# Layer 3 of a four-layer graph network: the pair's factors become the stationary operand of the sum over sources

## The chip, the cores and the metric

The kernel runs on one core of a Trainium2 chip. The metric is the device time of one execution in microseconds. A core has a matrix engine (TensorE, PE in the profile, with PEld for its weight loads), a vector engine (VectorE, DVE), a scalar engine for activation functions (ScalarE, ACT), a general engine (GpSimd, POOL), and queues that start DMA transfers (SP's above all). TensorE multiplies a stationary operand, loaded first (LDWEIGHTS), by a moving operand that is passed through it column by column; the result goes to PSUM, and the other engines read it from there.

## The reference

Four graph layers follow each other, each of the form x = x + layer(relu(layernorm(x)), adj), with 3327 nodes, 64 features and a dense 3327 x 3327 matrix adj in f32. Layer 0 is a gated recurrent layer applied twice, layer 1 a hyperbolic linear one, layer 2 a sum with weights that halve from neighbour to neighbour. The change is in layer 3:

```
x_tan = _logmap0(x, C)
left = x_tan @ att_W[:D] + att_b
right = x_tan @ att_W[D:]
adj_att = sigmoid(left + right.T) * adj
x_local = _logmap(x[:, None, :], x[None, :, :], C)
support_t = einsum('ij,ijd->id', adj_att, x_local)
return _proj(_expmap(x, support_t, C), C)
```

For target i and source j the term `_logmap(x_i, x_j)` is a factor that depends on the pair (i, j), times a combination of x_i and x_j. So the sum over j needs, for each target, two things: the factors times 64 features of x_j, and the factors times one number for each source.

## The kernel before

Nodes are padded to 3328, 26 blocks of 128. The first 13 blocks and the last 13 are kept side by side. Layers 0 to 2 come first (lines 142 to 485) and are not touched. Layer 3 works on **pairs**: `pairs` lists 26 of them, 13 for each half of the targets. A pair is one half of the targets (1664 of them, HN) and two blocks of sources, block c and block 13 + c, named b = 0 and b = 1. What is made for a pair is a tile `gl` of 128 sources by 2 x 1664 targets, f32: the pair's factors.

For each pair the engines do this. `load3` fetches the pair's part of adj (SP's queue). `distances(n, k)` runs on TensorE for half k of the targets: the two source blocks use the upper and the lower 64 rows of the array, and a bf16 matmul adds further terms. ScalarE then takes Gelu of the result into `gl` (L818) and Tanh for the attention into `th` (L825). `weights` multiplies by adj on VectorE (L845). `squares` is split between ScalarE (L836) and VectorE (L837). `products` multiplies both on VectorE in three pieces (L854), the first of which makes the whole of `gl[:, 0]`. Then comes the sum over sources on TensorE, in two functions. `gather` has the 64 features of a source block, scaled (`xd`), as its stationary operand and passes the factors, 416 targets at a time; the result has features on partitions and targets in columns, and two of them lie on the two halves of a PSUM bank (`accx0`, `accx1`). `gather_p` does the same with one column, `p2c`, and puts four rows into `accp`. Both add over the 13 pairs of a half.

After the last pair of a half, `collect` copies these sums into `half` (ScalarE and VectorE), turns them with 13 transposes on TensorE so that targets lie on partitions, and multiplies by `qs` into `sums`. `finish` then does the rest for that half on VectorE, with small steps; its steps for the first half are spread, four at a time, over the following pairs.

The order on each engine in layer 3 is the order in which the program writes the instructions (`manual_schedule`). The loop at lines 921 to 944 writes it by hand: for pair n, products of n, distances of n+1 (second half), gather of n, weights and squares of n+1, distances of n+2 (first half), gather_p of n. `gl` has three buffers, `th` and the tile of adj two; the PSUM tiles of the distances, `pta` and `ptb`, have one each.

Of the kernel before, what the change touches and what calls it, by code (L numbers as in the profile page):

```python
# [8 lines left out]
F32 = mybir.dt.float32  # L9
BF16 = mybir.dt.bfloat16  # L10
I32 = mybir.dt.int32
AF = mybir.ActivationFunctionType
OP = mybir.AluOpType
# [4 lines left out]
D = 64  # L18
P = 128
NB = 26  # L20
NP = NB * P
HB = NB // 2
HN = NP // 2
CH = 416
NQ = HN // CH
# [18 lines left out]
HG = -7.090763495839726  # L44
HK = 0.012618748686465375
HD = 0.7055609776434136 / HK
SQ = HN + 512


# [11 lines left out]
def gnn_kernel(ctx: ExitStack, tc: tile.TileContext, t, out):  # L61
    nc = tc.nc
    V, S, G, T = nc.vector, nc.scalar, nc.gpsimd, nc.tensor
# [7 lines left out]
    ident = const.tile([P, P], F32, name="ident")  # L71
# [9 lines left out]
    def small(pool, name):  # L81
        return pool.tile([P, NB], F32, name=name, tag=name)
# [59 lines left out]
    with ExitStack() as c012:  # L142
# [5 lines left out]
        ps_acc = c012.enter_context(tc.tile_pool(name="ps_acc", bufs=1, space=PSUM))  # L148
        pools = {}

        def scratch(name):
            return pools["ps"].tile([P, 512], F32, name=name, tag="ps")
# [42 lines left out]
        for n in ("1", "2"):  # L195
# [3 lines left out]
            b = nd.tile([P, 2, 3], F32, name="b" + n)  # L199
# [57 lines left out]
        def accumulators():  # L257
            return [ps_acc.tile([P, 512], F32, name=f"acc{q}", tag=f"acc{q}") for q in range(NQ)]
# [36 lines left out]
        with tc.tile_pool(name="gate", bufs=2) as gp:  # L295
            src = dst = h_t
            for (w, ih, hh, b, brz), order in zip(ggc, (UP, DOWN)):
# [3 lines left out]
                for q in range(NQ):  # L301
                    cs = slice(q * CH, (q + 1) * CH)
                    gates = []
                    for g in range(2):
                        p = scratch("gate")
# [10 lines left out]
                    n = gp.tile([P, CH], F32, name="n", tag="n")  # L316
# [72 lines left out]
        with ExitStack() as c2:  # L389
# [21 lines left out]
            for i in range(3):  # L411
                p = mk.tile([P, NB, D], BF16, name=f"part{i}", bufs=1)
# [6 lines left out]
            acc = accumulators()  # L419
            with tc.tile_pool(name="psc", bufs=2, space=PSUM) as psc, tc.manual_schedule():  # L420
# [19 lines left out]
                for j in reversed(range(NB)):  # L440
                    a = adj_block(j)
                    mask = mk.tile([P, NP], BF16, name="mask", tag="mask")
                    V.tensor_scalar(mask, a, 0.0, None, op0=OP.not_equal)  # L443
                    for k in range(NQ // 2):
                        ws = []
                        for h in range(2):
                            p = psc.tile([P, 2, 512], F32, name="cnt", tag="cnt")
                            for i in range(2):
# [3 lines left out]
                                    lhsT=tri,  # L452
                                    rhs=mask[:, i0 : i0 + CH],
                                    start=True,
                                    stop=behind is None,
                                )
                                if behind is not None:
                                    T.matmul(  # L458
                                        p[:, i, :CH],
                                        lhsT=ones,  # L460
                                        rhs=behind[:, i0 : i0 + CH],
                                        start=False,
                                        stop=True,
# [39 lines left out]
    n3 = c3.enter_context(tc.tile_pool(name="n3", bufs=1))  # L503
# [108 lines left out]
    sums = n3.tile([P, NB, D + 1], F32, name="sums")  # L612

    with ExitStack() as cf:
        f3 = cf.enter_context(tc.tile_pool(name="f3", bufs=1))
        wk = cf.enter_context(tc.tile_pool(name="wkf", bufs=2))
        ps_acc = cf.enter_context(tc.tile_pool(name="ps_accf", bufs=1, space=PSUM))
        ps = cf.enter_context(tc.tile_pool(name="psf", bufs=1, space=PSUM))
# [5 lines left out]
        pairs = [(hf, c) for hf in range(2) for c in range(HB)]  # L624
# [26 lines left out]
        last = f3.tile([P, 1], I32, name="last")  # L651
# [8 lines left out]
        q = small(n3, "q")  # L660
        V.tensor_scalar(q, x2, 0.5, -0.5, op0=OP.mult, op1=OP.add)
        V.reciprocal(q, q)
        xd = f3.tile([P, HB, 3, D], F32, name="xd")
# [10 lines left out]
        for n, (dst, a) in enumerate(((xs, 0), (xw, 1))):  # L674
            for c0 in range(0, HB, 8):
                m = min(8, HB - c0)
                p = pair_tile(n + c0 // 8).rearrange("p a b -> p (a b)")
# [38 lines left out]
        for i in range(3):  # L716
            b = f3.tile([P, 4, NB], BF16, name=f"part{i}")
# [20 lines left out]
        p = ps.tile([P, 1024], BF16, name="tr", tag="tr")  # L738
# [9 lines left out]
        for g in range(7):  # L748
            src = packt[:, g * P : (g + 1) * P]
# [9 lines left out]
        for i in range(4):  # L759
            p = pair_tile(i)  # L760
# [5 lines left out]
                p[:, :, :CH],  # L766
            )

        p2c = small(n3, "p2c")
        V.tensor_scalar(p2c, q, 2.0, 2.0, op0=OP.mult, op1=OP.add)  # L770
        qs = small(n3, "qs")
        V.tensor_scalar(qs, q, 0.125 * HK, None, op0=OP.mult)

# [3 lines left out]
        p = ps.tile([P, 512], F32, name="tr", tag="tr")  # L777
# [6 lines left out]
        gs, ths = {}, {}  # L784
# [48 lines left out]
        def squares(n):  # L833

            gl = gs[n].rearrange("p b n -> p (b n)")
            S.activation(gl[:, :SQ], gl[:, :SQ], AF.Square, bias=hg)  # L836
            V.scalar_tensor_tensor(  # L837
                gl[:, SQ:], gl[:, SQ:], 2 * HG, gl[:, SQ:], op0=OP.add, op1=OP.mult
            )
# [9 lines left out]
        def products(n):  # L849

            gl = gs[n].rearrange("p b n -> p (b n)")
            th = ths.pop(n).rearrange("p b n -> p (b n)")
            for lo, hi, hd in ((0, HN, HD), (HN, SQ, HD), (SQ, 2 * HN, HD + HG * HG)):
                V.scalar_tensor_tensor(  # L854
# [2 lines left out]

        acc = {}

        def gather(n):  # L860
            hf, c = pairs[n]
            if c == 0:
                for k in range(2):
                    acc[k] = ps_acc.tile([P, 512], F32, name=f"accx{k}", tag=f"accx{k}")
                acc["p"] = ps_acc.tile([P, 512], F32, name="accp", tag="accp")
            gl = gs[n]
            for b in range(2):
                first, last = c == 0 and b == 0, c == HB - 1 and b == 1
                for i in range(NQ):
                    T.matmul(  # L870
                        acc[i // 2][(i % 2) * D : (i % 2 + 1) * D, :CH],
                        lhsT=xd[:, c, b, :],
                        rhs=gl[:, b, i * CH : (i + 1) * CH],
                        start=first,
                        stop=last,
                    )

        def gather_p(n):
            hf, c = pairs[n]
            gl = gs.pop(n)  # L880
            for b in range(2):
                first, last = c == 0 and b == 0, c == HB - 1 and b == 1
                kk = 2 * c + b
                for i in range(NQ):
                    T.matmul(  # L885
                        acc["p"][32 * i : 32 * i + 1, :CH],
                        lhsT=p2c[:, kk : kk + 1],
                        rhs=gl[:, b, i * CH : (i + 1) * CH],
                        start=first,
                        stop=last,  # L890
                    )

        def collect(hf):
            half = f3.tile([D + 1, HN], F32, name="half", tag="half")
            for i in range(NQ):
                cs = slice(i * CH, (i + 1) * CH)
                src = acc[i // 2][(i % 2) * D : (i % 2 + 1) * D, :CH]
                srcp = acc["p"][32 * i : 32 * i + 1, :CH]
                S.activation(half[:D, cs], src, AF.Copy)
                V.tensor_copy(half[D : D + 1, cs], srcp)  # L900
            for c0 in range(0, HB, 6):
                n = min(6, HB - c0)
                p = ps.tile([P, 512], F32, name="tr", tag="tr")
                for c in range(n):
                    T.transpose(
                        p[:, c * (D + 1) : (c + 1) * (D + 1)],
                        half[:, (c0 + c) * P : (c0 + c + 1) * P],
                        ident[: D + 1, : D + 1],
                    )
                V.tensor_mul(  # L910
                    sums.rearrange("p (c a) d -> p c a d", a=2)[:, c0 : c0 + n, hf, :],
                    p[:, : n * (D + 1)].rearrange("p (c d) -> p c d", d=D + 1),
                    qs.rearrange("p (c a) -> p c a", a=2)[:, c0 : c0 + n, hf, None].to_broadcast(
                        [P, n, D + 1]
                    ),
                )
# [4 lines left out]
        for n in range(-2, len(pairs)):  # L921
            if n >= 0:
                products(n)
            if 0 <= n + 1 < len(pairs):
                distances(n + 1, 1)
            if n >= 0:
                gather(n)
            if 0 <= n + 1 < len(pairs):
                weights(n + 1)
                load3(n + 3)  # L930
                squares(n + 1)
            if n + 2 < len(pairs):
                begin(n + 2)
                distances(n + 2, 0)
            if n >= 0:
                gather_p(n)
                if pairs[n][1] == HB - 1:
                    hf = pairs[n][0]
                    collect(hf)
                    final = finish(hf)  # L940
            for _ in range(4):
                next(final, None)
            if n == 0:
                ok = nc.values_load(within, min_val=0, max_val=1)
# [4 lines left out]
    with ExitStack() as cg:  # L949
# [3 lines left out]
        ps_acc = cg.enter_context(tc.tile_pool(name="ps_acc3", bufs=1, space=PSUM))  # L953
        ps = cg.enter_context(tc.tile_pool(name="ps3", bufs=2, space=PSUM))
# [42 lines left out]
        for hf in range(2):  # L997
# [6 lines left out]
            for b0 in range(0, HB, 4):  # L1004
                bs = blocks[b0 : b0 + 4]
                p = scratch3(b0 // 4)
                for i, b in enumerate(bs):
                    k = slot(b)
# [5 lines left out]
            acc = [ps_acc.tile([P, 512], F32, name=f"ac{q}", tag=f"ac{q}") for q in range(NQ)]  # L1014
# [69 lines left out]
            for g in range(len(groups) + 1):  # L1084
                if g < len(groups):
                    for j in groups[g]:
                        n = hf * NB + j + 2
# [10 lines left out]
            half = g3.tile([D + 1, HN], F32, name="half", tag="half")  # L1098
            for q in range(NQ):
                S.activation(half[:, q * CH : (q + 1) * CH], acc[q][: D + 1, :CH], AF.Copy)  # L1100
            for c0 in range(0, HB, 6):
                n = min(6, HB - c0)
                p = scratch3(c0 // 6)
                for c in range(n):
# [10 lines left out]
                    op0=OP.mult,  # L1115
# [50 lines left out]
```

## Time and profile before

| | |
|---|---|
| three runs | 920.04, 920.91, 924.06 us; median 920.91 |
| the profiled execution | 922.38 us, of which the span from first to last instruction is 920.6 |
| busy in the span | PE 720.2, PEld 339.6, DVE 519.6, ACT 356.3, POOL 9.5 us |
| mean granted TensorE clock | 0.899 of full |
| layer 3's pairs | about 633 to 895 us, then finish to the end |
| weights L845 | 52 instructions of 1.89 us |
| distances L799 (f32), L810 (bf16) | 416 and 208 recorded passes of 416 columns |
| gather L870, gather_p L885 | 416 recorded passes each of 416 columns |
| transposes in collect L905 | 26, mean 278 ns |

The busy time of a matmul is from its start to a modelled end, so matmuls that follow each other in a pipeline overlap in it: how long TensorE is held by one is read from the start of one to the start of the next. The granted clock is the share of full speed that TensorE was allowed.

### The profile page before, as it was taken

The numbers are of one execution on the slowest core, as the hardware profiler recorded it, in microseconds if no ns is written. First come the engines' busy times: TensorE is split into PE (matmuls) and PEld (weight loads), VectorE is DVE, ScalarE is ACT, GpSimd is POOL, SyncE is SP. The second block draws the span as 40 slices with busy tenths as digits, with TensorE's granted clock in tenths as the row PEclk, the third lists the DMA queues.
The fourth block names the chain that finished last, engine by engine and source line by source line (L and its number), as shares of the span: only waits on it lengthen the run. The fifth ranks groups of instructions, "written<-read, shape, count | busy, mean of one in ns | idle before, by whom it ended". The sixth has DMA issues, their size and how long they took to land.

```text
span 920.6 us, 9670 instructions
## 1 busy us (share of the span) xinstructions
PE 720.2 (78%) x4043; PEld 339.6 (37%) x4043; DVE 519.6 (56%) x618; ACT 356.3 (39%) x361; POOL 9.5 (1%) x18
## 2 busy tenths in 40 slices
PE   0999998998953999505999999115899997699970
PEld 0644445443431444203444445112344442244420
DVE  4200025000189000796676675862899998899986
ACT  0000011000022000111666665012899995799961
POOL 1000000000000000000000002000000000000000
PEclk9999999999985999856999999556999997899995
DMA  8999930997000599500688610300465562445501
GB/s 274 378 379 429 404 122 21 384 359 275 0 1 0 209 385 373 221 0 1 253 330 310 243 53 1 151 3 10 149 223 176 197 222 80 159 159 217 200 24 22
DMA packets 25345, 170.22 MB, mean 185 GB/s; under 512 B 9165, under 2 KB 9293, under 8 KB 16077
## 3 DMA queue, kind: packets, MB, share of 16 engines
q1 hardware_dynamic: 21718, 168.88, 48.1%
q10 hardware_dynamic: 3575, 0.64, 0.4%
q8 instruction: 33, 0.54, 0.2%
q14 instruction: 19, 0.16, 0.1%
HBM read 168.40 MB, written 0.85 MB: 184 GB/s over the span
## 4 chain that ended last, share of the span: by engine, by line
PE 62%; DVE 19%; DMA 10%; issue 4%; ACT 3%; ACTq 1%; POOL 0%; SPq 0%; DVEq 0%; POOLq 0%
PE acc L261 28%; PE pt L799 9%; PE accx L870 8%; DMA adj<-in_adjT 6%; PE cnt L450 4%; PE cnt L458 4%; PE accp L885 3%; DMA res<-in_adjT 3%; PE pt L810 2%; DVE sq L86 1%; DVE gl L854 1%; PE lin L245 1%; ACT gl L818 1%; DVE n L88 1%; DMA w<-in_W 1%
## 5 line engine op out<-in xcount | busy, mean ns | idle before, releaser
L261 PE MATMUL acc<-adj,m_n 128*64 128x416 f32 x816 | 203.8, 523 | 9.4 <-DMA adj<-in_adjT 8.8
L261 PEld LDWEIGHTS acc<-adj,m_n 128*64 128x64 f32 x816 | 85.4, 138 | 109.7 <-issue 90.3
L261 PE MATMUL acc<-res,m_n 128*64 128x416 f32 x432 | 108.0, 523 | 22.8 <-DVE m_n L349 22.2
L466 ACT ACTIVATE w<-cnt,ebias 128x832 uint16<-128x832 f32 x104 | 93.4, 950 | 62.9 <-PE cnt L458 51.8
L278 DVE COPY m_t<-acc 128x416 f32<-128x416 f32 x12 | 6.2, 582 | 189.1 <-PE acc L261 189.1
L845 DVE SCALAR_TENSOR_TENSOR th<-th,adj 128x1664 f32<-128x1664 f32 x52 | 97.7, 1887 | 12.5 <-ACT th L825 12.4
L799 PE MATMUL pt<-xs 64*128 64x416 f32 x208 | 99.4, 559 | 5.4 <-ACT gl L818 5.4
L799 PE MATMUL pt<-xw,xs 64*128 64x416 f32 x208 | 100.5, 565 | 0.0
L854 DVE SCALAR_TENSOR_TENSOR gl<-gl,th 128x1664 f32<-128x1664 f32 (+2 forms) x78 | 97.6, 1305 | 0.0
L870 PE MATMUL accx<-gl,xd 128*64 128x416 f32 x416 | 83.2, 539 | 13.8 <-DVE gl L854 13.8
L818 ACT ACTIVATE gl<-pt 128x832 f32<-128x832 f32 x104 | 84.1, 861 | 24.3 <-PE pt L810 24.3
L825 ACT ACTIVATE th<-leftb,righth 128x1664 f32<-128x1664 f32 x52 | 87.6, 1685 | 0.0
L450 PE MATMUL cnt<-mask,tri 128*128 128x416 bf16 x208 | 70.8, 344 | 2.4 <-ACT w L466 1.0
L261 PEld LDWEIGHTS acc<-res,m_n 128*64 128x64 f32 x432 | 44.5, 138 | 68.4 <-issue 66.5
L261 PE MATMUL acc<-w,part 128*64 128x416 bf16 x624 | 66.1, 346 | 4.3 <-DVE part L413 4.3
L458 PE MATMUL cnt<-behind,ones 128*128 128x416 bf16 x192 | 65.1, 339 | 0.0
L476 DVE TENSOR_TENSOR behind<-behind,mask 128x3328 bf16<-128x3328 bf16 x23 | 43.5, 1892 | 36.0 <-PE cnt L458 36.0
L217 PE MATMUL tr<-ident,h_n 128*128 128x128 f32 x26 | 6.0, 423 | 62.4 <-DVE h_n L139 62.4
L836 ACT ACTIVATE gl<-gl,hg 128x2176 f32<-128x2176 f32 x26 | 54.8, 2106 | 0.0
L870 PEld LDWEIGHTS accx<-gl,xd 128*64 128x64 f32 x416 | 30.8, 141 | 62.1 <-DVE gl L854 33.4
L810 PE MATMUL pt<-rows_i,rows_j 64*128 64x416 bf16 x208 | 50.8, 347 | 0.0
L443 DVE TENSOR_SCALAR mask<-adj 128x3328 bf16<-128x3328 f32 x21 | 39.5, 1885 | 19.9 <-DMA adj<-in_adjT 13.3
(228 smaller groups left out, 645.4 us busy)
## 6 DMA issues: line engine op xcount, KB each, us to landing
adj<-in_adjT SPq DMA_DIRECT2D x89, 1664.0 KB
res<-in_adjT SPq DMA_DIRECT2D x9, 1664.0 KB
xn<-in_x SPq DMA_DIRECT2D x1, 832.0 KB
out<-w SPq DMA_DIRECT2D x2, 416.0 KB
ih<-in_wihT ACTq DMA_DIRECT2D x4, 48.0 KB
hh<-in_whhT ACTq DMA_DIRECT2D x4, 48.0 KB
w<-in_W ACTq DMA_DIRECT2D x4, 16.0 KB
attw<-in_att_W SPq DMA_DIRECT2D x1, 64.0 KB
```

The source lines that it names most:

```text
L261: T.matmul(acc[q][h * D : (h + 1) * D, :CH], lhsT=lhsT, rhs=rhs, start=first, stop=last)
L450: T.matmul(p[:, i, :CH], lhsT=tri, rhs=mask[:, i0 : i0 + CH], start=True, stop=behind is None,)
L458: T.matmul(p[:, i, :CH], lhsT=ones, rhs=behind[:, i0 : i0 + CH], start=False, stop=True,)
L466: S.activation(w, p[:, :, :CH], AF.Relu, bias=ebias, scale=-EXP_UNIT)
L799: T.matmul(pts[b][:, i, :CH], lhsT=xs[rs, c * P : (c + 1) * P], rhs=rhs[rs, q0 : q0 + CH], start=True, stop=False,)
L810: T.matmul(pts[b][:, i, :CH], lhsT=rows_j[rs, j0 : j0 + P], rhs=rows_i[rs, i0 : i0 + CH], start=False, stop=True,)
L818: S.activation(gs[n][:, b, 2 * k * CH : (2 * k + 2) * CH].rearrange("p (i n) -> p i n", i=2), pts[b][:, :, :CH], AF.Gelu, scale=-HA,)
L825: S.activation(ths[n][:, k, :], leftb[:, hf * HN : (hf + 1) * HN], AF.Tanh, bias=righth[:, kk : kk + 1], scale=0.5,)
L836: S.activation(gl[:, :SQ], gl[:, :SQ], AF.Square, bias=hg)
L845: V.scalar_tensor_tensor(th[:, b, :], th[:, b, :], 1.0, a[:, b, :], op0=OP.add, op1=OP.mult)
L854: V.scalar_tensor_tensor(gl[:, lo:hi], gl[:, lo:hi], hd, th[:, lo:hi], op0=OP.add, op1=OP.mult)
L870: T.matmul(acc[i // 2][(i % 2) * D : (i % 2 + 1) * D, :CH], lhsT=xd[:, c, b, :], rhs=gl[:, b, i * CH : (i + 1) * CH], start=first, stop=last,)
```

## The change

A new tile `xp` holds for each source block the 64 features and, as a 65th column, the factor that was `p2c`. `gather` and `gather_p` are replaced by `sum_targets(n, b)`, called once for each source block of the pair, at the two places in the loop where they stood. It has 128 columns of the pair's factors (128 sources by 128 targets) as the stationary operand and passes the 65 columns of `xp`, 13 times for the 13 target blocks of a half. The result has targets on partitions. Seven target blocks share one PSUM bank (`accx0`), six the other (`accx1`); the start flag is given for the first block in each bank. `collect` has no copies and no transposes: it multiplies the two banks by `qs` into `sums`. The copy into `xp` is made by GpSimd.

```diff
-        p2c = small(n3, "p2c")
-        V.tensor_scalar(p2c, q, 2.0, 2.0, op0=OP.mult, op1=OP.add)
+        xp = f3.tile([P, NB, D + 1], F32, name="xp")
+        G.tensor_copy(
+            xp[:, :, :D].rearrange("p (c a) d -> p c a d", a=2), xd[:, :, :2, :]
+        )
+        V.tensor_scalar(xp[:, :, D], q, 2.0, 2.0, op0=OP.mult, op1=OP.add)
...
-        def gather(n):
...
-        def gather_p(n):
...
+        def sum_targets(n, b):
             hf, c = pairs[n]
-            if c == 0:
+            if c == 0 and b == 0:
                 for k in range(2):
...
+                    acc[k] = ps_acc.tile([P, BANK_BLOCKS, D + 1], F32, name=f"accx{k}", tag=f"accx{k}")
+            gl = gs[n] if b == 0 else gs.pop(n)
+            for i in range(HB):
+                T.matmul(
+                    acc[i // BANK_BLOCKS][:, i % BANK_BLOCKS, :],
+                    lhsT=gl[:, b, i * P : (i + 1) * P],
+                    rhs=xp[:, 2 * c + b, :],
+                    start=c == 0 and b == 0 and i % BANK_BLOCKS == 0,
+                    stop=c == HB - 1 and b == 1,
+                    skip_group_check=True,
+                )
 
         def collect(hf):
-            half = f3.tile([D + 1, HN], F32, name="half", tag="half")
...
+            for k in range(2):
+                cs = slice(k * BANK_BLOCKS, min(HB, (k + 1) * BANK_BLOCKS))
+                n = cs.stop - cs.start
                 V.tensor_mul(
...
+                    sums.rearrange("p (c a) d -> p c a d", a=2)[:, cs, hf, :],
+                    acc[k][:, :n, :],
...
             if n >= 0:
-                gather(n)
+                sum_targets(n, 0)
...
             if n >= 0:
-                gather_p(n)
+                sum_targets(n, 1)
```

## The prediction

> **What bounds the kernel now.** The change lies in layer 3, so the shares of the whole span say little. I read first the groups of instructions from 650 to 900 us with shapes kept apart, then the busy time by window, then the order of time of one pair, then the waits (from 660 to 756 us ACT waits 4.0 us in all for distances, DVE for nothing).
>
> The groups of the two gathers (columns: busy us, mean ns of one, idle before and what ended it):
>
> ```profile
> L870 PE MATMUL accx<-gl,xd 128*64 128x416 f32 x416 | 83.2, 539 | 13.8 <-DVE gl L854 13.8
> L870 PEld LDWEIGHTS accx<-gl,xd 128*64 128x64 f32 x416 | 30.8, 141 | 62.1 <-DVE gl L854 33.4 <-issue 28.3
> L885 PE MATMUL accp<-gl,p2c 128*1 128x416 f32 x416 | 41.0, 511 | 0.0
> ```
>
> 26 pairs times 8 matmuls are 208, but 416 are recorded: an f32 matmul is issued as two passes, each with its own weight load. Now the windows: one pair in the steady part, the middle of the layer, and a stretch of layer 0 (columns: length, then busy us of PE, PEld, DVE, ACT, POOL, granted clock, DMA share, GB/s).
>
> ```profile
> 60.00:120.00 60.00, 59.33 (x246) 25.72 (x243) 0.00 (x0) 0.00 (x0) 0.00 (x0) 1.00 0.99 411
> 705.13:713.75 8.62, 8.62 (x57) 3.68 (x56) 8.62 (x7) 8.26 (x8) 0.00 (x0) 1.00 0.57 203
> 763.40:773.80 10.40, 5.86 (x25) 3.06 (x25) 7.70 (x19) 5.37 (x9) 0.00 (x0) 0.67 0.41 155
> ```
>
> A pair takes 8.62 us, and DVE has no idle time in it: two weights (L845, 3.63 us), one square (L837, 1.27), three products (L854, 3.68), counted from start to start. ACT works 8.26 and waits 0.36. PE also shows 8.62, but that is latency; its streaming time must come from starts. These rows give them (start, length, engine):
>
> ```profile
> 713.78 3.03 PE L870 MATMUL accx<-gl,xd 128*64 128x416 f32 x16
> 716.74 0.61 PE L799 MATMUL pt<-xs 64*128 64x416 f32 x1
> 717.20 0.51 PE L799 MATMUL pt<-xs 64*128 64x416 f32 x1
> 717.55 0.34 PE L810 MATMUL pt<-rows_i,rows_j 64*128 64x416 bf16 x2
> 718.69 1.58 PE L885 MATMUL accp<-gl,p2c 128*1 128x416 f32 x16
> 720.20 0.61 PE L799 MATMUL pt<-xs 64*128 64x416 f32 x1
> ```
>
> From 717.20 to 717.55 is one f32 pass of 416 columns, 0.35 us. The gather holds PE from 713.78 to 716.74, 2.96 us for 16 passes: two run side by side (64 output rows each), 8 x 0.347 = 2.78 plus 0.18. The factor row holds it from 718.69 to 720.20, 1.51: four side by side, 4 x 0.347 = 1.39 plus 0.12. A half of the distances takes 1.95 where ACT does not hold it (716.74 to 718.69), with 1.73 of passes. So PE needs 2 x 1.95 + 2.96 + 1.51 = 8.37 of 8.62 us: **DVE bounds the pair, but PE has only 0.25 us to spare.** That is what the reader is to take from the rows: a near tie of three engines.
>
> **What the Trainium skill says.** TensorE: Matmul & The Clock Gate, section LDWEIGHTS, prices a weight load at columns / 1.2 ns, whatever the rows: 107 ns for 128 columns, 53 for 64. The trace agrees with this for f32: the first pass after a switch is followed by the next after 0.46 us where 128 columns are loaded (716.74 to 717.20), after 0.40 where 64 are, after 0.35 for one column; less the 0.35 of the pass, 0.11, 0.05 and 0. The same page, section Back-to-back issue gap, says that the spacing in a stream of load and matmul is set by both, overlapped; it has 81 ns at N=128, of no stated type. Here the trace differs and decides: layer 0's linear, f32, 128 columns loaded and 128 passed, at full clock, is
>
> ```profile
> 28.59 1.28 PE L245 MATMUL lin<-w,h_t 128*128 128x128 f32 x10
> ```
>
> (1.28 - 0.275 of the last) / 9 = 112 ns: load and pass lie on each other, neither is added. TensorEngine Tiling (Array Packing), section Key Properties, says that a change of tiling mode drains the array; I read the 0.12 left over in gather and factor row as that.
>
> **The change, part by part.** (1) Removed from every pair: 2.96 + 1.51 = 4.47 us of PE. (2) Added: 2 x 13 matmuls with 128 weight columns and 65 moving columns, so 52 loads and 52 passes. A pass of 65 columns is 0.347 x 65 / 416 = 54 ns, its load 107: the load is the longer, and no other tile of the array shares the time. That loads stay overlapped when they are longer than the pass is shown by the closing transposes, whose 128-column load goes through faster, with a pass of 65 columns:
>
> ```profile
> 898.50 0.45 PEld L905 LDWEIGHTS tr<-ident,half 65*128 65x128 f32 x6 [1.56 <-issue]
> ```
>
> (0.45 - 0.144) / 5 = 61 ns[...]. I take 112 ns for each of the 26 passes in a call of sum_targets, plus 0.12 drain and 0.11 for the first load, which nothing hides: 2.90 + 0.23 = **3.1 us a call**. Bounds: 107 ns and the drain alone, 2.9; 125 ns (a few more for each swap of weights), 3.5. (3) A pair on PE is then 2 x 1.95 + 2 x 3.1 = **10.1 us**; nothing on DVE (8.62) or ACT (8.26) covers it, so PE becomes the bound by 1.48 us over now. Does a wait come on top? Count from the end of distances(n+1, 1). ACT does Gelu 1.6, Tanh 1.6, Square 2.0 and is free at 5.2; PE finishes sum and the next distances at 3.1 + 1.95 = 5.05; its second sum ends at 8.2, when the PSUM tiles of the distances were read by 6.8. DVE's first product is ready at about 7.0, wanted at 10.1. So PE runs through; products are late for nobody.
> (4) The loads of adj (L632) are asked for every 10.1 us instead of 8.62 with a DMA share of 0.57: easier. The copy into xp on POOL is 1664 elements, twice L670's 0.88 us, on an idle queue at about 595 us, first read at 653: nothing. p2c's DVE operation becomes one of the same size, 0.17 us.
> (5) The ends of the halves: eight ACT copies, eight DVE copies, 26 transposes and six multiplies become four multiplies. At the end now, from 895.36 (factor row done) to 900.47 (first step of finish): 5.1 us; after, the wait of about 0.2 and multiplies of 455 and 390 columns at 0.6 each (the 390 take 0.56 today), 1.4. **Gain 3.7.** In the middle, from 763.40 to the first products of the second half at 773.77 is 10.4; after, 1.4 plus finish's first steps, 4.2, is 5.6. Of the 4.8 won I keep 4.5: PE's clock is down after its idle time there (0.67 in the row above), and the sum then pays for it.
>
> **The sum.** Gather 0 to gather 12 now 653.4 to 756.9: 12 steps, 12 x 1.48 = +17.8. Gather 12 to 15, 47.1 us now: the second sum ends 8.15 after gather 12 begins instead of 6.5, +1.65, less 4.5: about -3. DVE, ACT's table loads and finish bind there as now. To gather 16, 9.1 now: +1.0. Gather 16 to 24, eight steps: +11.8. From gather 24 to PE's last pass, 13.2 now: distances of pair 25 are done, Gelu, Tanh and Square (5.2), then L837 and one product (about 3) let sum 25 begin at 8.3, and two calls end at 14.5: +1.3. The end: -3.7. In all +25. Against the profiled execution (922.4 us, span 920.6) that is 947; its time is 1.5 us over the median of the three runs, so against 920.9 it is **946 us**.
>
> **Rivals.** *Load and pass in series.* If a load can't run beside a short pass, one takes 107 + 54 + 4 = 165 ns, a call 4.5 us, the pair 12.9: 2.8 x 23 pairs = 64 more, 1010 us. For it: no row has this load with so short an f32 pass. Against: both rows of streams above. 10 in 100. *The clock falls.* Passes would stream 3.47 + 2.8 = 6.3 of 10.1 us, 62%; in layer 0 from 60 to 120 us, 246 recorded passes two at a time are 246 x 0.174 = 43 us, 71%, at clock 1.00. At half clock in the sums alone a pair is near 16, some 1080 us. 3 in 100. *Loads go through faster* (the other side): the closing transposes load 128 columns in 61 ns. At that pace a call is 26 x 0.061 + 0.23 = 1.8, PE needs 7.5, DVE stays the bound at 8.62, and only the ends count: -3.7 - 4.5, so 913 us. The point that decides is a call of 2.36 us, 82 ns a pass. Against it stands the exposed 0.11 us of ordinary f32 loads. 8 in 100; between the two, within 0.5%, 3 in 100. *It doesn't do what it says*: seven sums share a bank with one start flag; PSUM — Partial Sum Buffer, section The four PSUM rules, says that the start clears the bank's bits and later first writes overwrite, so the counts stand; no run here shows it. Not priced.
>
> **Numbers.** My case has 76 in 100, 935 to 965 of its own (the bounds 2.9 and 3.5 us move 23 pairs by -9 and +18). The range 934 to 972 leaves out the faster case and most of the serial and slow-clock ones. About 0.5% is what a measurement of this kernel can tell from no change. Faster 0.08, same 0.03, slower 0.89.
>
> **What would show it.** In the profile after: a group of 1352 passes of 65 columns with as many loads, starts 107 to 115 ns apart; the pair's period 9.7 to 10.5 with DVE idle about 1.5 us in it, ended by PE or ACT, and ACT waiting for distances; from PE's last pass to finish under 2 us. A period of 8.6 with DVE full shows the fast load; one near 13 the series; a granted clock under 0.9 from 660 to 760 the third.

## The result, and the profile after

Four runs of the changed kernel took 946.15 to 959.33 us, median 950.75; four of the kernel before 920.04 to 924.96, median 922.48. The ratio is 1.0317, with a 95% interval of 1.0237 to 1.0397: **slower by about 3%**. The profiled execution took 951.16 us, its span 949.4, against 920.6 before.

Layers 0 to 2 are the same in both kernels but end at slightly different times in each profile (the first wide VectorE step of layer 3 starts between 573 and 582 us). I therefore also give **layer 3's own length**, from the start of that step (layernorm's subtraction, written to `xc`) to the end of the span: 920.6 - 578.6 = 342.0 us before, 949.4 - 577.5 = 371.9 after, **+29.9**. A second profile of the changed kernel gives 946.9 - 575.1 = 371.8, so this measure repeats where the whole span does not.

The groups of the new sum, from 640 to 935 us (busy us, mean ns of one, idle before and what ended most of it):

```profile
L873 PE MATMUL accx<-xp,gl 128*128 128x65 f32 x1352 | 172.3, 288 | 12.4 <-DVE gl L858 12.4
L873 PEld LDWEIGHTS accx<-xp,gl 128*128 128x128 f32 x1352 | 165.3, 202 | 38.5 <-issue 28.2 <-DVE gl L858 8.8 <-DVE w L604 1.0
```

There are 1352 passes, as counted, each with a load of its own. In the windows of one pair, of the two stretches in the middle and of the end, the columns are as before (length, PE, PEld, DVE, ACT, POOL, granted clock, DMA share, GB/s):

```profile
715.63:725.62 9.99, 9.99 (x79) 7.70 (x77) 8.63 (x7) 8.26 (x8) 0.00 (x0) 1.00 0.49 172
775.60:785.50 9.90, 5.04 (x41) 3.86 (x39) 8.66 (x17) 9.07 (x9) 0.00 (x0) 0.88 0.49 173
785.50:812.00 26.50, 21.27 (x108) 17.32 (x110) 21.89 (x47) 11.59 (x12) 0.00 (x0) 0.69 0.23 72
906.00:929.00 23.00, 20.29 (x126) 18.82 (x124) 12.69 (x11) 6.46 (x5) 0.00 (x0) 0.72 0.01 1
```

The pair now takes 9.99 us instead of 8.62. VectorE and ScalarE have the same work in it as before, 8.63 and 8.26 us, but no longer fill it. The waits from 660 to 756 us name what they wait for (waiting engine and line, releaser, us in total, times, longest):

```profile
ACT gl L822 <- PE pt L814: 17.4, 10, 1.8
DVE th L849 <- ACT th L829: 13.7, 10, 1.5
```

ScalarE waits 1.74 us in each pair for the distances from TensorE, where it waited 0.36, and VectorE 1.37 us behind ScalarE, where it waited for nothing. That is how a bound that has moved to TensorE shows itself, though TensorE's busy time filled the pair before the change too. In order of time, TensorE's rows of one call and of the end are (start, length, engine):

```profile
720.61 2.98 PEld L873 LDWEIGHTS accx<-xp,gl 128*128 128x128 f32 x26 [0.52 <-issue]
908.91 6.02 PE L873 MATMUL accx<-xp,gl 128*128 128x65 f32 x52
917.25 11.36 PE L873 MATMUL accx<-xp,gl 128*128 128x65 f32 x52 [2.31 <-DVE gl L858]
```

In the first row 26 loads start (2.98 - 0.19) / 25 = 112 ns apart. The other two rows are the same work, two calls one after the other, for the last pair but one and for the last pair. The second takes nearly twice as long. This was not in the forecast. The windows of the gap of 2.31 us before it and of the calls themselves show the clock:

```profile
914.94:917.25 2.31, 0.00 (x1) 0.01 (x1) 2.31 (x3) 0.00 (x0) 0.00 (x0) 0.80 0.00 0
917.25:928.61 11.36, 11.36 (x52) 11.17 (x52) 2.44 (x3) 0.00 (x0) 0.00 (x0) 0.50 0.01 1
```

It fell within the gap and stayed at half to the last pass. The second profile of the changed kernel has the same two figures, 0.80 and 0.50.

### The profile page after: what moved, and what is told of

The parts are those of the page before. It is cut to its first block, busy times and chain, and to the rows that moved or that the text cites. A ratio compares the mean times of both kernels' runs of the same rounds, so it can differ in the third digit from the quotient of the medians.

```text
span 949.4 us, 10637 instructions
## 1 busy us (share of the span) xinstructions
PE 762.2 (80%) x4537; PEld 452.7 (48%) x4537; DVE 515.0 (54%) x608; ACT 352.4 (37%) x353; POOL 11.1 (1%) x19
## 5 line engine op out<-in xcount | busy, mean ns | idle before, releaser
L262 PE MATMUL acc<-adj,m_n 128*64 128x416 f32 x816 | 206.5, 521 | 6.8 <-DMA adj<-in_adjT 5.9
L873 PEld LDWEIGHTS accx<-xp,gl 128*128 128x128 f32 x1352 | 165.3, 202 | 38.5 <-issue 28.2
L873 PE MATMUL accx<-xp,gl 128*128 128x65 f32 x1352 | 172.3, 288 | 12.4 <-DVE gl L858 12.4
L803 PE MATMUL pt<-xs 64*128 64x416 f32 x208 | 101.7, 571 | 3.7 <-ACT gl L822 3.7
L444 DVE TENSOR_SCALAR mask<-adj 128x3328 bf16<-128x3328 f32 x21 | 39.5, 1886 | 22.4 <-DMA adj<-in_adjT 14.5
L262 PEld LDWEIGHTS <-part 128*64 128x64 bf16 x624 | 31.6, 111 | 36.6 <-issue 19.2
```

What stands on the lines that cost most here:

```text
L262: T.matmul(acc[q][h * D : (h + 1) * D, :CH], lhsT=lhsT, rhs=rhs, start=first, stop=last)
L803: T.matmul(pts[b][:, i, :CH], lhsT=xs[rs, c * P : (c + 1) * P], rhs=rhs[rs, q0 : q0 + CH], start=True, stop=False,)
L873: T.matmul(acc[i // BANK_BLOCKS][:, i % BANK_BLOCKS, :], lhsT=gl[:, b, i * P : (i + 1) * P], rhs=xp[:, 2 * c + b, :], start=c == 0 and b = ...
```

## The experiments

Layer 3's length stands behind each time. It came to 371.9 and 371.8 us in the two profiles of the changed kernel; of each of the other kernels there is one profile.

**1. Fewer columns moved.** Theory: the weight load sets the pace of the passes. Rival: the moved columns do.

```diff
-                    acc[i // BANK_BLOCKS][:, i % BANK_BLOCKS, :],
+                    acc[i // BANK_BLOCKS][:, i % BANK_BLOCKS, 32:],
...
-                    rhs=xp[:, 2 * c + b, :],
+                    rhs=xp[:, 2 * c + b, 32:],
```

> Leaves out 32 of the 64 features in the sums (33 columns are moved instead of 65; the loads stay). Theory: the 128-column weight load sets the pace of the sum, so 26 passes still take 2.9 us, a call 3.05 us, the pair 10.0 us, time within 3 us of the changed kernel's 951. Rival, the moved columns set the pace (111 ns for 65 columns): 33 columns give 56 ns, a call about 1.6 us, VectorE becomes the bound again at 8.6 us a pair, some 915 us.

Measured: 1005 and 1028 us in two runs, layer 3 444.0 us in the slower one, so the forecast of the time was missed by far; the two runs differ too much for a ratio. Over the whole execution the mean granted clock was 0.833 and 0.818 in them, against 0.892 to 0.896 in the four runs of the changed kernel. The profile (windows from 656 to 720 and 720 to 750 us, and loads in order of time) has both an answer and a surprise:

```profile
656.00:720.00 64.00, 64.00 (x343) 44.99 (x342) 39.01 (x28) 38.67 (x32) 0.00 (x0) 0.69 0.32 115
720.00:750.00 30.00, 30.00 (x224) 23.29 (x222) 24.25 (x18) 23.69 (x21) 0.00 (x0) 0.96 0.48 171
726.05 2.98 PEld L874 LDWEIGHTS accx<-xp,gl 128*128 128x128 f32 x26 [0.52 <-issue]
```

While the clock is up, the loads' 2.98 us are those of 65 columns to the hundredth: half the columns, the same pace. The moved columns do not set it. But the clock is often down: 0.69 from 656 to 720 us, 0.72 from 656 to 1006 us, where the pairs lie (0.94 in the changed kernel, from its first sum to its last pass). TensorE is busy all the same, so fewer columns made the kernel slower by the clock that it was granted. Three windows of 3.41 us that follow each other show how the clock comes and goes:

```profile
701.06:704.48 3.42, 3.42 (x32) 3.19 (x30) 0.00 (x0) 3.14 (x4) 0.00 (x0) 1.00 0.00 0
704.48:707.89 3.41, 3.41 (x13) 1.17 (x11) 3.33 (x3) 2.05 (x2) 0.00 (x0) 0.50 0.22 36
707.89:711.30 3.41, 3.41 (x30) 3.25 (x30) 3.41 (x3) 3.19 (x3) 0.00 (x0) 1.00 0.91 345
```

The first and the third hold little but one call of the sum, the second the distances between them. After the call the clock is halved, after the distances it is back, and TensorE is busy in all three.

**2. More columns moved.** The same question from the other side; 31 features are moved a second time and their sums not used.

```diff
-BANK_BLOCKS = 7
+BANK_BLOCKS = 5
...
-        xp = f3.tile([P, NB, D + 1], F32, name="xp")
+        xp = f3.tile([P, NB, 96], F32, name="xp")
...
```

> 96 columns are moved instead of 65 (31 more, whose sums are not used; the sums lie in three banks, five target blocks in each). Theory of the load: a pass of 96 columns is 80 ns, still under the 107 of the load, so a call stays at 3.05 to 3.15 us, the pair at 10.0, time 951 give or take 3. Rival, moved columns set the pace: 164 ns a pass, a call 4.4 us, the pair 12.7, about 1012 us. Rival, load and pass partly in series: each pass longer by up to 26 ns, a call 3.7 us, about 980 us.

Measured: 942.4 us, ratio to before 1.0236 (1.0198 to 1.0273); layer 3 364.5 us, 7.4 **less** than with 65 columns, which was not expected either. The pace of the loads is unchanged (2.98 us for 26), the pair 10.04 us: the load theory again, and no part in series. The gain lies at the end and in the middle. The end, in order of time, and the window of the gap in it:

```profile
904.82 6.04 PE L876 MATMUL accx<-xp,gl 128*128 128x96 f32 x52
913.16 6.04 PE L876 MATMUL accx<-xp,gl 128*128 128x96 f32 x52 [2.29 <-DVE gl L861]
910.87:913.16 2.29, 0.00 (x0) 0.00 (x0) 2.29 (x3) 0.00 (x0) 0.00 (x0) 1.00 0.00 0
```

After the same idle time, 2.29 us, the clock is still up, and the last two calls take 6.04 us and not 11.36. In the middle the first sums of pairs 13 and 14 take 5.3 and 5.1 us instead of 5.8, and pair 12 to 15 takes 44.2 us instead of 48.4.

**3. Half the columns loaded.** Only 64 of the 128 factor columns are stationary; half of the targets are left out.

```diff
-                    lhsT=gl[:, b, i * P : (i + 1) * P],
+                    lhsT=gl[:, b, i * P : i * P + D],
```

> Leaves out half of the targets: only 64 of each block's 128 factor columns are loaded as stationary operand; all 65 columns are moved, the number of loads and passes stays. Theory of the load: a load is 53 ns, a pass 54, the pace 56 to 62 ns, a call about 1.75 us; TensorE needs 7.4 us a pair, less than VectorE's 8.62, so the pair falls back to 8.6 us and the time to 910 to 918 us, under the kernel before. Rival, a floor of about 111 ns for each f32 pass whatever is loaded: nothing changes, 951 us.

Measured: 906.2 us, ratio 0.984 (0.980 to 0.988), 4 us under the forecast band; layer 3 330.7 us. The passes start 58 ns apart ((1.59 - 0.14) / 25, from the loads of a call), a call takes 1.73 us with its last pass's latency, VectorE's products start 8.63 us apart. So 111 ns is no floor of an f32 pass: it goes with the number of columns **loaded**. Which of the two sets the 58 ns this run does not tell, since a load of 64 columns and a pass of 65 are of one length by the prediction's working (53 and 54 ns).

**4. The gap at the end filled.** Theory: the last two calls are slow because TensorE stood idle for 2.3 us before them.

```diff
+            if n == len(pairs) - 1:
+                p = pair_tile(0)
+                for _ in range(12):
+                    T.matmul(p[:, 0, :CH], lhsT=identb, rhs=rows_i[:, :CH], start=True, stop=True)
```

> Adds 12 bf16 matmuls of 416 columns (2.1 us, result unused) just before the last pair's two sums, where TensorE stood idle for 2.3 us. In the profile of the changed kernel those two sums took 11.4 us, half speed, where two in the steady part take 6.1. Theory, the idle time pulled the clock down: with the gap filled the clock stays up, the two sums take 6.1 us, 5 us less, some 946 us. Rival, load-bound passes without distances between them don't keep the clock up: it falls during or before these sums all the same, and no more than 1 to 3 us are won.

Measured: 945.8 us (ratio 1.0253, 1.0193 to 1.0312), layer 3 366.2 us, 5.7 less. The intervals of the ratios of this and of the changed kernel overlap, so the gain rests on the profiles. In order of time:

```profile
917.28 2.27 PE L905 MATMUL pt<-rows_i,identb 128*128 128x416 bf16 x12
919.76 6.02 PE L873 MATMUL accx<-xp,gl 128*128 128x65 f32 x52 [0.21 <-DVE gl L858]
```

The two calls take 6.02 us at full speed. The theory holds and its rival falls: load-bound passes of 65 columns do keep a clock that is up, for these 6 us; what they did not do in the changed kernel was to bring it up again.

**5. All three gaps filled.** As in 4, with 26 and 28 filling matmuls before the first sums of pairs 13 and 14. The changed kernel was run once more beside it.

```diff
+            fill = {HB: 26, HB + 1: 28, len(pairs) - 1: 12}.get(n, 0)
...
```

> The changed kernel once more, on the chip and beside the runs of before that the next two kernels are compared with. Both theories: pair 10.0 us, the last two sums 11.4 us at half clock, 946 to 955 us.

> Fills TensorE's three idle stretches of layer 3 with bf16 matmuls whose result is not used: 26 and 28 of them (4.5 and 4.8 us) before the first sums of pairs 13 and 14, 12 before the last pair's. Theory: the two middle sums, 5.8 us each at half clock, fall to 3.1, the distances behind them from 3.0 to 2.0, the last two sums from 11.4 to 6.1. That is 5.3 us at the end and some 5 in the middle, 10 in all under the changed kernel on this chip, about 940. Rival: VectorE and ScalarE set the middle anyway (finish's small steps), so only the end's 5 us are won, about 946.

Measured: the changed kernel 948.4 us (ratio 1.0291, 1.0257 to 1.0324), with the gaps filled 937.4 (1.0205, 1.0161 to 1.0249). In layer 3 it is 363.1 against 371.8, 8.7 less: if 5.7 of it is the end, as in run 4, **3.0 is the middle**, less than the 5 expected. The first sums of pairs 13 and 14 fell to 3.1 us each, but that of pair 15 now came after a gap of 1.4 us and took 4.5.

**6. The load split over the two column halves of the array.** If loads set the pace, the way out is not fewer columns moved but loads side by side. Each 128-column load becomes two of 64; the result is the whole one.

```diff
-                T.matmul(
-                    acc[i // BANK_BLOCKS][:, i % BANK_BLOCKS, :],
-                    lhsT=gl[:, b, i * P : (i + 1) * P],
+                for s in range(2):
+                    T.matmul(
+                        acc[i // BANK_BLOCKS][s * D : (s + 1) * D, i % BANK_BLOCKS, :],
+                        lhsT=gl[:, b, i * P + s * D : i * P + (s + 1) * D],
...
```

> The whole sum, but each 128-column load split into two 64-column loads in the two column halves of the array, with 65 columns moved through each: twice the loads and passes, the same result. Theory: loads of different column halves run beside each other, as the old gather's passes did; a load is 53 ns and a pass 54, so a pair of them takes about 60 ns, a call 1.75 us like the run with half of the columns left out, VectorE bounds the pair at 8.6 us, time 904 to 912, under the kernel before by 1 to 1.7%. Rival, there is one path for loads and they follow each other: 52 loads of 58 ns make 3.0 us, a call 3.1 to 3.2, nothing won, 950 us. Rival, each instruction costs a floor near 58 ns however it is tiled: the same as that, 950 us.

Measured: 908.9 us, ratio **0.987 (0.984 to 0.990)**: faster than the kernel before by 1.3%. Layer 3 takes 329.5 us, 12.5 less than before the change and 42.4 less than after it. Its loads from 640 to 910 us, two calls in order of time, and the window of one pair:

```profile
L874 PEld LDWEIGHTS accx<-xp,gl 128*64 128x64 f32 x2704 | 87.6, 144 | 51.3 <-DVE gl L858 32.9 <-DVE th L849 11.4 <-issue 7.1
694.89 1.60 PEld L874 LDWEIGHTS accx<-xp,gl 128*64 128x64 f32 x52 [0.52 <-DVE gl L858]
703.52 1.60 PEld L874 LDWEIGHTS accx<-xp,gl 128*64 128x64 f32 x52 [0.52 <-DVE gl L858]
690.00:698.60 8.60, 8.02 (x130) 5.40 (x132) 8.60 (x7) 8.24 (x8) 0.00 (x0) 1.00 0.55 200
```

Twice as many loads (2704) take less time in all: 52 start within 1.60 us, one every 29 ns, where one column half alone had one every 58 (run 3). Loads of different column halves run beside each other. The two calls, of one pair and the next, are 8.63 us apart, TensorE waits for VectorE's products before each, and VectorE is busy throughout the window: it is the bound again.

**7. Both together.** The column halves with 26, 33 and 28 filling matmuls in the gaps.

> The sum in two column halves, with TensorE's idle stretches filled as well (26, 33 and 28 bf16 matmuls, results not used, before the first sums of pairs 13 and 14 and the last pair's). Theory: the clock stays up; the last two sums fall from 5.4 to 3.3 us, the two middle ones from 3.1 to 1.8, of which perhaps 1 to 2 us reach the end of the middle: 3 to 4 us under the run with column halves, about 905. Rival: with VectorE as the bound only the end counts, 2 us, and in the noise.

Measured: 902.9 us, ratio 0.983 (0.980 to 0.987). Layer 3 takes 328.3 us, 1.2 under run 6; the rest of the difference between the two profiled executions lies in the layers before, which are the same in both, and the intervals of the two ratios overlap. The last two sums fell from 5.4 to 3.3 us as expected, the two middle ones to 1.7, but the first sum of pair 15, after a gap of 4.1 us, took 3.1. The 3 to 4 us did not come; the rival (only the end counts, in the noise) is closer.

## Why the prediction was right, and which of its terms were not

The forecast was 946 us, slower, from +25 us on the profiled execution; measured were 950.75 us and +29.9 us in layer 3. The mechanism (the load sets the pace, TensorE becomes the bound) was right, and so was its price, the pair. What was taken for the clock after an idle stretch was not.

*The pace of a pass.* Taken at 112 ns, from layer 0's linear; measured 112. That row loads 128 columns and passes 128, so by itself it did not tell which of the two sets the pace; runs 1 and 2 do. The page of the Trainium skill that prices a load by its columns (TensorE: Matmul & The Clock Gate, LDWEIGHTS) agrees with the runs: 128 loaded columns keep the pace of 112 ns with 33, 65 and 96 moved columns, and with 64 loaded it is 58 ns. The series rival (165 ns a pass) is refuted by every call. The fast-load rival is refuted for ordinary f32 loads: the closing transposes, with 61 ns for 128 columns, are no measure for them. For the same reason they were no witness that a load longer than its pass stays overlapped, as the prediction has it; the sum's own rows are.

*A call.* Taken at 3.1 us, measured 3.04 (715.62 to 718.66). *The distances.* Taken at 1.95, measured 1.95 (718.66 to 720.61). *The pair.* Taken at 10.1, measured 9.99. No wait came on top, as worked out.

The sum, term by term (us; before and after by the starts of the first sum of each pair):

| term | predicted | measured |
|---|---|---|
| layer 3's beginning to pair 0 | 0 | 74.8 to 73.1: -1.7 |
| pair 0 to 12 | +17.8 | 103.5 to 119.9: +16.4 |
| pair 12 to 15, the middle | -3 | 47.1 to 48.4: **+1.3** |
| pair 15 to 16 | +1.0 | 9.1 to 10.0: +0.9 |
| pair 16 to 24 | +11.8 | 69.0 to 79.9: +10.9 |
| pair 24 to the last pass | +1.3 | 13.2 to 19.7: **+6.5** |
| from there to finish | -3.7 | 5.1 to 0.6: -4.5 |
| all of layer 3 | +25 | +29.9 |

The total is nearer than its terms: the middle and the tail came out 9.5 us over the forecast, the others 4.9 us under it in all. That these partly cancel is luck.

**The term that failed is the tail**, and with it the middle: the step "two calls end at 14.5" took both last calls at full clock. The start at 8.3 us after the first sum of pair 24 was right (908.91 to 917.25), but the two calls took 11.36 instead of 6.2. Run 4 shows the cause, the idle 2.3 us: with them filled, layer 3 loses 5.7 us, more than the whole error of this term. In the middle I kept 4.5 of 4.8 us; two sums at half clock cost 2.7 us each, and filling their gaps gives back 3.0 of the 4.3 us by which this term was off; the rest stays open. At the end one thing helped more than counted: the first bank's multiply runs while the second is still summed, so that only 0.6 us follow the last pass where 1.4 had been taken.

The beginning, -1.7 us, was not predicted and no run was made for it.

*The clock rival.* I gave it 3 in 100 and argued from the streaming share, 62% against 71% in a part of layer 0 at full clock. For the steady part that was right (clock 1.00). But it came true in the three places where TensorE first stands idle, and run 1 shows how near the edge the whole was: at 33 columns the streaming share of a pair is (3.47 + 52 x 0.0275) / 10 = 49% by the same working, and the clock of the pairs falls to 0.72. The skill's page describes a monitor that releases the clock after a window of about 3.4 us of activity (section What's actually happening). Here 11.4 us of uninterrupted load-bound passes did not release it. My estimate for these, 54 ns of pass in 111, is a streaming share of 49%; with 80 in 111 (run 2) the clock after the same gap was up.

The traces tell more. In all ten of them the granted clock is 0.50 or 1.00 and changes only on a grid of 3.41 us, which agrees with the length of that window. For every window of the grid in layer 3 (from 640 us on, to 1010 in run 1 and 930 in the others) the streaming share can be estimated from the starts of the passes, with 0.347 us for 416 f32 columns, half of it for bf16, and twice as long at half clock:

| clock in the window | streaming share | windows | clock in the next window |
|---|---|---|---|
| full | under 34% | 55 | half after all 55 |
| full | 42% and more | 621 | full after all 621 |
| half | under 70% | 87 | half after all 87 |
| half | 80% and more | 45 | full after 43 |

The 36 windows between these bounds went both ways. How busy TensorE looks does not separate them: in 28 of the windows after which the clock fell, all of run 1, it was busy throughout, and so it was in 11 of the other runs' windows after which the clock stayed at half. So in these runs the clock follows the share of time in which columns stream, window by window, and keeping it takes far less than getting it back. The share is an estimate, and no run sets it by itself. A call of 65 columns, 49%, keeps a clock that is up and can't bring it back; one of 33, about 25%, loses it. The prediction's mean over a pair was the wrong measure, though it gave the right answer for the steady part. It also matters where the grid lies: the gap of the changed kernel's end fell into one window, with 26% of streaming, that of run 2 into two, with 35% and 55%.

*The faster rival's time.* 913 us was worked out for VectorE as the bound. Runs 3 and 6, where it is the bound, give 906 and 909: layer 3 of run 6 is 12.5 us shorter than before, where 8.2 had been taken for the ends. The middle (pair 12 to 15) gives 5.8 of it where 4.5 had been counted, and 1.8 are the unexplained beginning.

## What to carry to other kernels

In these runs an f32 matmul with more stationary columns than moving ones cost what its load costs, so compare loaded columns with moved columns before swapping operands; 128 against 65 made the load the bound. If the load is the bound, split it over column halves of the array: the loads then ran side by side, and the same swap turned from 3% slower to 1.3% faster. And look at what TensorE does just after an idle stretch: load-bound passes may not bring the clock back, so a gap can cost more than its own length (here 2.3 us cost another 5.3). Count the share of streaming over stretches as short as the clock's window, not over the whole loop.

## What the runs showed of the hardware that I had not expected

Loads of 64 f32 columns into the two column halves overlap: 52 start in 1.60 us, one every 29 ns, against one every 58 ns into one half.

Moving fewer columns can make a kernel slower. With 33, 65 and 96 moved columns and the same loads, layer 3 took 444, 372 and 364 us (the first is one profile of two runs that differ by 22 us); the pace of the loads at full clock is the same in all three, the mean granted clock over the pairs 0.72, 0.94 and 0.97.

A gap of 2.3 us was enough to lose the clock for the next 11.4 us with 65 columns, in both profiles, and cost nothing with 96 columns, in the one profile there is. By that estimate the clock follows the share of streaming in windows of 3.41 us, and a TensorE that is busy throughout can lose it.
